# Edge stage of a graph layer on one Trainium2 core: edges sorted on the chip by tile of targets, sums in SBUF, a hand-ordered pipeline of quads and pairs

## The chip, the cores and the metric

One core of a Trainium2 chip runs the whole program. TensorE (PE), VectorE (DVE), ScalarE (ACT), GpSimd (POOL) and SyncE (SP) each work through a list of instructions of their own, in order, and wait for each other by semaphores. SP, ACT and POOL issue DMAs; only POOL issues the indirect ones, in which an index per partition chooses a row in DRAM. The metric is the device time of one execution in microseconds (us), the median of several runs.

## What is computed

x holds 3125 nodes of 512 features; 50000 edges run from src to dst (edge attributes: 32 numbers, and 4 called sh). Three parts follow each other: x plus a graph layer plus a linear attention, both of layernorm(x); then x plus a mixture of 8 experts (2 for each node). The graph layer's edge part, cut to what matters:

```python
pre = irrep_linear(x, W_pre0, b_pre0, W_pre1)          # p0: 128, p1: 3 x 128 features
ip1 = einsum('eum,eum->eu', p1[edge_dst], p1[edge_src]) / 3.0
s0 = concatenate([p0[edge_dst], p0[edge_dst], ip1], -1)
w = ssp(edge_attr @ W_f1) @ W_f2 * (ssp(s0 @ W_s1) @ W_s2)   # ssp: softplus - log 2; 4 x 128
x0e, x1e = split_irreps(x[edge_src]);  sh0, sh1 = edge_sh[:, 0], edge_sh[:, 1:4]
out0 = w1 * x0e * sh0 + w4 * (sum(x1e * sh1) / sqrt(3.0))
out1 = w2 * x0e * sh1 + w3 * x1e * sh0
out = segment_sum(merge(out0, out1), edge_dst, 3125) + self_x
```

(The layer is called with edge_index = (src, dst), so the program's src is the row that an edge adds to, its target, and dst the row that it reads.)

## The kernel before, in words

The program has three stages, each in a block with pools of its own: the dense stage (L121), the edge stage (L357) and the expert stage (L502). A scheduler orders the instructions of each engine. N is 3125 (NT = 25 tiles of 128 nodes), T is 392 tiles of 128 edges.

**Dense stage.** x is loaded into `base`, normalised and transposed into xT (L177 to L185); POOL adds a bias to base (L182). POOL also zeroes the sums in DRAM (L196) and copies the expert weights into row order (w_rows, 32 DMAs of 1 MB, L207). Then, in chunks of 512 nodes, each tile gets a row `r` of 1312 numbers (L256 to L277): p0 through W_s1 (32), p1 (384) and the node's own transformed features (512). They are written to two DRAM tables: rows_d (416 numbers, read by target) and rows_s (896, read by source); the own features also start the sums acc[0]. The loop of keys and values follows (ps_k, ps_v, ps_kv, L292 to L307; POOL's memset of v at L302), then queries, z and the output projection (L318 to L352).

**Edge stage.** 98 groups of G = 4 edge tiles. For each tile POOL gathers 128 rows of rows_d (gd, L400) and of rows_s (gx, L404). A group compares its targets with each other (sel, L416) and moves repeated targets of a tile to spare rows (at, L425). DVE multiplies p1 of both ends (prod, L429); PE transposes and adds the products by 12 matmuls with the identity (ps_ip, L433) and makes both hidden layers (ps_h, L442 to L446); ACT and DVE apply ssp (hid, L454). For each tile then: two matmuls of 32 rows by 512 (wa L460, wb L462), the weights wt (L465 to L467), the features ft on DVE (L472 to L486), a matmul with sel that adds edges of one target (ps_s, L491), a copy to `so`, and an indirect DMA that adds so to one of two DRAM accumulators (L494).

**Expert stage.** Both accumulators are loaded and added (ac, L569), projected and added to base; then come the gates, the sorting of tokens by expert, and 56 slots of 128 tokens (L798 to L846).

Of the kernel before, what the change touches and what calls it, by code (L numbers as in the profile page):

```python
# [8 lines left out]
F32 = mybir.dt.float32  # L9
# [9 lines left out]
MUL = 128  # L19
G = 4  # L20
NACC = 2
# [14 lines left out]
def gnn_mix_moe_kernel(ctx: ExitStack, tc: tile.TileContext, a: dict, out: bass.AP):  # L36
# [11 lines left out]
    NPAD = (N + P + P - 1) // P * P  # L48
# [11 lines left out]
    keep = ctx.enter_context(tc.tile_pool(name="keep", bufs=1))  # L60
    dram = ctx.enter_context(tc.tile_pool(name="dram", bufs=1, space=DRAM))


    base = keep.tile([P, NT, D], F32, name="base")
    nc.vector.memset(base[:, NT - 1, :], 0.0)
    for t in range(NT):
        nc.sync.dma_start(base[: tn(t), t, :], a["x"][t * P : t * P + tn(t), :])
# [6 lines left out]
    before = const.tile([P, P], F32, name="before")  # L74
    nc.vector.tensor_scalar(before, jp, 0.0, None, op0=ALU.is_lt)
# [3 lines left out]
    nc.vector.memset(half, 0.5)  # L79

# [3 lines left out]
    acc = [dram.tile([NPAD, D], F32, name=f"acc{k}") for k in range(NACC)]  # L84
# [4 lines left out]
    def layer_norm_stats(pool):  # L89

        mv = pool.tile([P, NT, 2], F32, name="mv")
        nc.vector.memset(mv, 1.0)
        for t in range(NT):
            n = tn(t)
            st = pool.tile([P, 6], F32, name="bn", bufs=3)
            nc.vector.bn_stats(st[:n], base[:n, t, :])
            nc.vector.bn_aggr(mv[:n, t, :], st[:n])
        rs = pool.tile([P, NT], F32, name="rs")
        nc.scalar.activation(rs, mv[:, :, 1], AF.Sqrt, bias=eps)
        nc.vector.reciprocal(rs, rs)  # L100
        return mv, rs

    def normalise(dst, t, mv, rs):
        n = tn(t)
        nc.vector.tensor_scalar(
            dst[:n], base[:n, t, :], mv[:n, t, 0:1], rs[:n, t : t + 1],
            op0=ALU.subtract, op1=ALU.mult,
        )

    def transpose_rows(dst, src, t, psum):  # L110

        n = tn(t)
        ps = psum.tile([P, 4, P], F32, name="ps_t", tag="mm")
        for b in range(4):
            nc.tensor.transpose(ps[:, b, :n], src[:n, b * P : (b + 1) * P], ident[:n, :n])
        nc.scalar.copy(dst[:, :, t * P : t * P + n], ps[:, :, :n])
# [4 lines left out]
    with ExitStack() as c1:  # L121
        w = c1.enter_context(tc.tile_pool(name="w1", bufs=1))
        big = c1.enter_context(tc.tile_pool(name="big1", bufs=1))
        work = c1.enter_context(tc.tile_pool(name="work1", bufs=2))
        psum = c1.enter_context(tc.tile_pool(name="psum1", bufs=4, space=PSUM))
# [51 lines left out]
        mv, rs = layer_norm_stats(w)  # L177
        for t in range(NT):
            n = tn(t)
            xn = work.tile([P, D], F32, name="xn")  # L180
            normalise(xn, t, mv, rs)
            added = nc.gpsimd.tensor_add(base[:n, t, :], base[:n, t, :], b_add[:n])  # L182
            nc.vector.tensor_add(base[:n, t, :], base[:n, t, :], xn[:n])
            transpose_rows(xT, xn, t, psum)

        zero = w.tile([P, 2 * D], F32, name="zero")
        nc.gpsimd.memset(zero, 0.0)
        with tc.issue_after(added.ins):  # L190
            for k in range(NACC):
                r0 = N if k == 0 else 0
                while r0 < NPAD:
                    left = NPAD - r0
                    n, r = (min(2 * P, left), 2) if left % 2 == 0 else (1, 1)
                    nc.gpsimd.dma_start(  # L196
                        acc[k][r0 : r0 + n, :].rearrange("(p r) d -> p (r d)", r=r),
                        zero[: n // r, : r * D],
                    )
                    r0 += n  # L200


        with tc.issue_after(added.ins):
            for e in range(NE):
                for l in range(NL + 1):
                    src = a["Wh"][e, l] if l < NL else a["Wo"][e]
                    nc.gpsimd.dma_start(  # L207
                        w_rows[l][e * P : (e + 1) * P, :].rearrange("p (k f) -> p k f", k=4),
                        src.rearrange("(k p) f -> p k f", p=P),
                    )  # L210
# [3 lines left out]
        for c in range(NCH):  # L214
            m = cn(c)
            cols = slice(c * CH, c * CH + m)
            sq = work.tile([P, 3, CH], F32, name="sq", tag="wide")
            nc.vector.tensor_mul(sq[:, :, :m], xT[:, 1:4, cols], xT[:, 1:4, cols])
            nc.vector.tensor_add(sq[:, 0, :m], sq[:, 0, :m], sq[:, 1, :m])
            nc.vector.tensor_add(sq[:, 0, :m], sq[:, 0, :m], sq[:, 2, :m])  # L220
            rooted = nc.scalar.activation(n1[:, cols], sq[:, 0, :m], AF.Sqrt, scale=1.0 / 3.0)


        for c in range(NCH):
# [27 lines left out]
            for t in tiles_of(c):  # L252
# [24 lines left out]
                nc.sync.dma_start(acc[0][rows, :], r[:n, x0:])  # L277
# [40 lines left out]
        for c in range(NCH):  # L318
# [10 lines left out]
            for t in tiles_of(c):  # L329
# [12 lines left out]
                )  # L342
                pt = psum.tile([P, 4, P], F32, name="ps_zt", tag="mm")
# [8 lines left out]
                nc.vector.tensor_add(base[:n, t, :], base[:n, t, :], po[:n])  # L352
# [3 lines left out]

    with ExitStack() as c2:  # L357
        w = c2.enter_context(tc.tile_pool(name="w2", bufs=1))
        gat = c2.enter_context(tc.tile_pool(name="gat", bufs=3))
        work = c2.enter_context(tc.tile_pool(name="work2", bufs=2))  # L360
        ps1 = c2.enter_context(tc.tile_pool(name="ps1", bufs=1, space=PSUM))
        ps2 = c2.enter_context(tc.tile_pool(name="ps2", bufs=2, space=PSUM))


        to_i = w.tile([P, T], I32, name="to_i")
        nc.sync.dma_start(to_i, a["src_t"])
        of_i = w.tile([P, T], I32, name="of_i")
        nc.sync.dma_start(of_i, a["dst_t"])
        sh = w.tile([P, T, 4], F32, name="sh")
        nc.sync.dma_start(sh, a["sh_t"])  # L370
        w_f1 = w.tile([HID, HID], F32, name="w_f1")
        nc.scalar.dma_start(w_f1, a["W_f1"])
        w_s1c = w.tile([P, HID], F32, name="w_s1c")
        nc.scalar.dma_start(w_s1c, a["W_s1"][2 * MUL :, :])

        w_fs = w.tile([2 * HID, D], F32, name="w_fs")
        nc.scalar.dma_start(w_fs[:HID], a["W_f2"])
        nc.scalar.dma_start(w_fs[HID:], a["W_s2"])

        to_f = w.tile([P, T], F32, name="to_f")  # L380
        nc.vector.tensor_copy(to_f, to_i)

        spare_i = w.tile([P, 1], I32, name="spare_i")
        nc.gpsimd.iota(spare_i, pattern=[[0, 1]], base=N, channel_multiplier=1)
        spare = w.tile([P, 1], F32, name="spare")
        nc.vector.tensor_copy(spare, spare_i)
        away = w.tile([P, T], F32, name="away")
        nc.vector.tensor_scalar(away, to_f, spare, -1.0, op0=ALU.subtract, op1=ALU.mult)
# [4 lines left out]
        isq3 = 1.0 / math.sqrt(3.0)  # L393
        for g in range(T // G):
            gs = slice(g * G, (g + 1) * G)
            gd = gat.tile([P, G, HID + 3 * MUL], F32, name="gd")
            gx = gat.tile([P, G, 3 * MUL + D], F32, name="gx")
            for i in range(G):
                t = g * G + i
                nc.gpsimd.indirect_dma_start(  # L400
                    out=gd[:, i, :], out_offset=None, in_=rows_d[:, :],
                    in_offset=bass.IndirectOffsetOnAxis(ap=to_i[:, t : t + 1], axis=0),
                )
                nc.gpsimd.indirect_dma_start(  # L404
                    out=gx[:, i, :], out_offset=None, in_=rows_s[:, :],
                    in_offset=bass.IndirectOffsetOnAxis(ap=of_i[:, t : t + 1], axis=0),
                )
            row = gat.tile([P, G, P], I32, name="row")
            nc.sync.dma_start(row.rearrange("p g j -> p (g j)"), _rows(a["src_row"][g * G * P :], P, G * P))
            ea = gat.tile([HID, G * P], F32, name="ea")  # L410
            nc.sync.dma_start(ea, a["edge_attr"][:, g * G * P : (g + 1) * G * P])

            sel = work.tile([P, G, P], F32, name="sel")
            nc.vector.tensor_tensor(  # L416
                sel, row, to_f[:, gs].unsqueeze(2).to_broadcast([P, G, P]), op=ALU.is_equal
            )
            dup = work.tile([P, G, P], F32, name="dup")
            nc.vector.tensor_mul(dup, sel, before.unsqueeze(1).to_broadcast([P, G, P]))  # L420
            cnt = work.tile([P, G], F32, name="cnt")
            nc.vector.tensor_reduce(cnt, dup, AX.X, ALU.add)
            nc.vector.scalar_tensor_tensor(cnt, cnt, 0.0, away[:, gs], op0=ALU.is_gt, op1=ALU.mult)
            at = work.tile([P, G], I32, name="at", bufs=3)
            nc.vector.tensor_add(at, cnt, to_f[:, gs])  # L425


            prod = work.tile([P, G, 3 * MUL], F32, name="prod")
# [511 lines left out]
```

## Time and profile before

| what | us |
|---|---|
| median of 3 runs (3865.62 to 3876.13) | 3869.45 |
| the profiled execution, its own time | 3855.79 |
| its span, first to last instruction | 3854.0 |
| dense stage: start to the last output projection (L351) | 0 to 643.5 |
| first gather of the edge stage (L400) | 646.1 |
| first and last indirect add to DRAM (L494) | 693.8, 2791.7 |
| expert stage: first matmul (L572), first of the slots (L820) | 2801.9, 3009.6 |

How to read the profile: the page gives each engine's busy time, the span in 40 slices (a digit is a busy share in tenths; PEclk is the TensorE clock that was granted, in tenths of full speed), and groups of instructions with their line, count, busy time, mean ns of one, and the idle time just before them with what ended it ("issue": nothing that the profile shows). "x392" is a count; "PEld" is TensorE's loading of a stationary operand. DMA-issuing on POOL counts as busy only for the indirect and direct DMAs' own instructions.

### The profile page before, as it was taken

To read this page: it belongs to the slowest core of one execution; us is meant where nothing else is said; L and a number is where in the kernel's file an instruction comes from. 1 tells how busy PE (TensorE), PEld (TensorE's weight loads), DVE (VectorE), ACT (ScalarE), POOL (GpSimd) and SP (SyncE) were. 2 spreads that over 40 slices of the span, in tenths; PEclk is the share of its full clock that TensorE was granted. 3 is DMA by queue.
4 is the path that set the end of the run, shared out by engine and by line. 5 is a ranking of instruction groups with operands and counts; after the bars stand their busy time and mean duration, and the time that the engine had idled before them with its cause. 6 is when DMAs were issued, how large, how long until landed. Compare 5 with 4: busy or idle time off the path is not lost. (4 is left out here: it accounts for less than half of the span.)

```text
span 3854.0 us, 45302 instructions
## 1 busy us (share of the span) xinstructions
PE 3360.6 (87%) x14722; PEld 2072.1 (54%) x14722; DVE 2199.5 (57%) x6167; ACT 1153.5 (30%) x2596; POOL 2192.2 (57%) x1678
## 2 busy tenths in 40 slices
PE   3579986889898989898989898989857899999998
PEld 2346543444444444444444444444442788888887
DVE  6311233688787888787878787878774222222221
ACT  1111110344444444444444444444310111111111
POOL 3300002688888878888887788887601344444442
PEclk8789998677777777777777777777775899999999
DMA  3790002678888888887878878888655215184550
GB/s 123 283 362 17 0 0 97 157 178 193 185 188 191 187 195 188 194 189 191 187 191 187 195 182 197 188 193 184 128 166 222 62 53 184 53 320 154 194 185 23
DMA packets 222731, 632.23 MB, mean 164 GB/s; under 512 B 53019, under 2 KB 57936, under 8 KB 211744
## 3 DMA queue, kind: packets, MB, share of 16 engines
q0 software_dynamic: 169328, 535.41, 53.5%
q1 hardware_dynamic: 43978, 81.76, 6.7%
q10 hardware_dynamic: 9190, 12.18, 0.9%
q8 instruction: 117, 1.92, 0.2%
q14 instruction: 118, 0.97, 0.1%
HBM read 619.43 MB, written 193.83 MB: 211 GB/s over the span
## 5 line engine op out<-in xcount | busy, mean ns | idle before, releaser
L494 POOL DMA_INDIRECT acc<-so,at x392 | 804.8, 2053 | 198.5 <-issue 119.9
L460 PE MATMUL wa<-w_fs,hid 32*128 32x512 f32 x784 | 648.8, 999 | 201.0 <-issue 104.0
L462 PE MATMUL wb<-w_fs,hid 32*128 32x512 f32 x784 | 712.0, 1038 | 1.7
L491 PE MATMUL ps_s<-ft,sel 128*128 128x512 f32 x784 | 542.5, 781 | 0.9 <-DVE ft L486 0.9
L404 POOL DMA_INDIRECT gx<-rows_s,of_i x392 | 469.1, 1197 | 119.5 <-issue 74.7
L400 POOL DMA_INDIRECT gd<-rows_d,to_i x392 | 434.4, 1108 | 124.0 <-issue 107.0
L433 PEld LDWEIGHTS ps_ip<-ident,prod 128*128 128x128 f32 x2352 | 395.1, 248 | 169.9 <-issue 169.9
L460 PEld LDWEIGHTS wa<-w_fs,hid 32*128 32x128 f32 x784 | 206.2, 274 | 518.0 <-issue 301.5
L829 DVE TENSOR_SCALAR h<-ps_f,bias 128x128 f32<-128x128 f32 x336 | 117.1, 350 | 558.1 <-PE ps_f L820 541.3
L772 POOL DMA_INDIRECT we<-w_rows,w_at x224 | 230.6, 1030 | 349.3 <-PE ps_f L820 130.3
L820 PE MATMUL ps_f<-h,we 128*128 128x128 f32 x3584 | 424.1, 277 | 4.0 <-ACT h L827 4.0
L820 PEld LDWEIGHTS ps_f<-h,we 128*128 128x128 f32 x3584 | 408.8, 192 | 7.5 <-ACT h L827 6.1
L493 ACT COPY so<-ps_s 128x512 f32<-128x512 f32 x392 | 227.7, 581 | 559.7 <-PE ps_s L491 524.5
L433 PE MATMUL ps_ip<-ident,prod 128*128 128x128 f32 x2352 | 384.4, 328 | 11.2 <-DMA ea<-in_edge_attr 8.3
L486 DVE SCALAR_TENSOR_TENSOR ft<-wt,sh,ft 128x128 f32<-128x128 f32 x1176 | 340.1, 343 | 0.0
L827 ACT ACTIVATE h<-ps_f,bias 128x128 f32<-128x128 f32 x336 | 121.4, 367 | 663.9 <-PE ps_f L820 570.5
L465 ACT ACTIVATE wt<-wa,sh 128x256 f32<-128x256 f32 x392 | 186.5, 476 | 424.1 <-PE wb L462 197.7
L473 DVE SCALAR_TENSOR_TENSOR dot<-gx,sh,dot 128x128 f32<-128x128 f32 x392 | 135.0, 344 | 259.1 <-ACT dot L472 91.7
L491 PEld LDWEIGHTS ps_s<-ft,sel 128*128 128x128 f32 x784 | 145.7, 232 | 249.6 <-DVE ft L479 114.3
L467 DVE TENSOR_TENSOR wt<-wt,wb 128x512 f32<-128x512 f32 x392 | 265.5, 677 | 5.4 <-PE wb L462 2.9
L462 PEld LDWEIGHTS wb<-w_fs,hid 32*128 32x128 f32 x784 | 185.2, 275 | 103.7 <-DVE wt L467 90.1
L820 PEld LDWEIGHTS ps_f<-xt,we 128*128 128x128 f32 x1792 | 210.5, 193 | 27.5 <-issue 27.0
(237 smaller groups left out, 4791.9 us busy)
## 6 DMA issues: line engine op xcount, KB each, us to landing
row<-in_src_row SPq DMA_DIRECT2D x98, 256.0 KB
w_rows<-in_Wh POOLq DMA_DIRECT2D x24, 1024.0 KB
ac<-acc SPq DMA_DIRECT2D x48, 256.0 KB
rows_s<-r SPq DMA_DIRECT2D x24, 448.0 KB
w_rows<-in_Wo POOLq DMA_DIRECT2D x8, 1024.0 KB
acc<-zero POOLq DMA_DIRECT2D x13, 512.0 KB
ea<-in_edge_attr SPq DMA_DIRECT2D x98, 64.0 KB
gd<-rows_d,to_i POOLq DMA_INDIRECT x392
```

The lines of the kernel that those rows point to most:

```text
L400: nc.gpsimd.indirect_dma_start(out=gd[:, i, :], out_offset=None, in_=rows_d[:, :], in_offset=bass.IndirectOffsetOnAxis(ap=to_i[:, t : t + ...
L404: nc.gpsimd.indirect_dma_start(out=gx[:, i, :], out_offset=None, in_=rows_s[:, :], in_offset=bass.IndirectOffsetOnAxis(ap=of_i[:, t : t + ...
L433: nc.tensor.matmul(ps_ip[:, i * P : (i + 1) * P], prod[:, i, b * P : (b + 1) * P], ident, start=(b == 0), stop=(b == 2),)
L460: nc.tensor.matmul(wa, hid[:HID, es], w_fs[:HID], start=True, stop=True)
L462: nc.tensor.matmul(wb, hid[HID:, es], w_fs[HID:], start=True, stop=True)
L467: nc.vector.tensor_mul(wt, wt, wb)
L486: nc.vector.scalar_tensor_tensor(ft[:, b, :], w2, sh[:, t, b : b + 1], ft[:, b, :], op0=ALU.mult, op1=ALU.add)
L491: nc.tensor.matmul(ps_s, sel[:, i, :], ft.rearrange("p b u -> p (b u)"), start=True, stop=True)
L493: nc.scalar.copy(so, ps_s)
L494: nc.gpsimd.indirect_dma_start(out=acc[i % NACC][:, :], out_offset=bass.IndirectOffsetOnAxis(ap=at[:, i : i + 1], axis=0), in_=so, in_offs ...
L772: nc.gpsimd.indirect_dma_start(out=dst, out_offset=None, in_=src, in_offset=bass.IndirectOffsetOnAxis(ap=at[:, j : j + 1], axis=0), bounds ...
L820: nc.tensor.matmul(pss[f], ws[l][:, k, f * P : (f + 1) * P], h[:, k, :], start=(k == 0), stop=(k == 3))
```

## The change

Edges are sorted into slots by tile of targets at the start of the dense stage: DVE counts the edges of each tile of 128 targets (25 compares and 25 scans over 392 columns), PE adds over partitions, and DVE works out a place for every edge. Each tile starts on a new pair (2 x 128 slots); NPR = 220 pairs, or NQ = 110 quads of 512 slots, cover the worst case, empty slots being zero. For each of 14 chunks of 28 edge tiles, a record of 40 numbers per edge is built (sh, both row numbers, place in the tile, and ssp(edge_attr @ W_f1)), and POOL puts each tile of records to its slots in DRAM by an indirect DMA (392 puts, after 10 DMAs that clear the records). The record tiles have two buffers. base is no longer kept: x plus its norm goes to `out` and is loaded again (y). The w_rows DMAs go from POOL's queue to SP's. In the edge stage all edges of a pair belong to one tile of 128 targets, so the one-hot matmul yields sums for that tile, which DVE adds to `acc` in SBUF at a tile number read from pair_tile; the indirect adds to DRAM and the search for repeated targets are gone. The products go to POOL, three multiplies of each tile from DVE to ACT, and the features of a tile take two matmuls instead of one. The order of PE, ACT, DVE and POOL in this stage is written out by hand. In the expert stage, own features and x come by two loads in place of the two accumulators'.

In the built order of instructions, POOL's 392 puts all stand ahead of its 25 memsets of v. On DVE the record writes of all 14 chunks stand ahead of the row stage's second chunk (xg, r), the layernorm of x between those of chunks 2 to 9. On PE the row stage, keys and values, and queries follow each other as before.

```diff
+    NPR = (T * P - NT) // (PR * P) + NT
+    NQ = (NPR * PR + G - 1) // G
...
+            rec = chk.tile([P, CT, REC], F32, name="rec")      # chk: bufs=2
...
+            for i in range(CT):
+                put = nc.gpsimd.indirect_dma_start(
+                    out=recs[:, :], out_offset=bass.IndirectOffsetOnAxis(ap=at_i[:, t : t + 1], axis=0),
+                    in_=rec[:, i, :], in_offset=None,
+                )
...
-                    nc.gpsimd.dma_start(
-                        w_rows[l][e * P : (e + 1) * P, :].rearrange("p (k f) -> p k f", k=4),
+                nc.sync.dma_start(
+                    w_rows[l][e * P : (e + 1) * P, :].rearrange("p (k f) -> p k f", k=4),
...
-                nc.sync.dma_start(acc[0][rows, :], r[:n, x0:])
...
+    acc = keep.tile([P, NT, D], F32, name="acc")
...
+        def fetch(q, k):                       # rec by SP; gd: bufs=3, gx: bufs=5
+            for i in (2 * k, 2 * k + 1):       # two indirect DMAs on POOL for each tile
+                nc.gpsimd.indirect_dma_start(
+                    out=Q.gd[:, (i + 2) % G, :], out_offset=None, in_=rows_d[:, :],
+                    in_offset=bass.IndirectOffsetOnAxis(ap=reci[:, i, 5:6], axis=0),
+                )
...
+        def products(q):
+            for k in range(2):
+                g = slice(2 * k, 2 * k + 2)
+                nc.gpsimd.tensor_mul(
+                    Q.prod[:, g, :], Q.gd[:, g, HID:], Q.gx[:, 2 - 2 * k : 4 - 2 * k, : 3 * MUL]
+                )
+        def turn(q):                           # 12 transposes into ps_ip, adding; ACT copies to ip
+        def hidden(q):                         # 4 matmuls, ip stationary, w_s1c moving (32 columns)
+            nc.vector.tensor_copy(Q.h1, Q.rec[:, :, 8:])
+            nc.vector.tensor_add(Q.h, ps, Q.gd[:, :, :HID])
+        def softplus(q):                       # Abs, Exp, Ln on ACT over 128 columns; one op on DVE
+        def turn_hidden(q):                    # 2 transposes; ACT copies to hT
+        def weigh(s):
+            wa = ps_w.tile([P, PR, D], F32, name="wa")         # ps_w: bufs=1
+            wb = ps_w.tile([P, PR, D], F32, name="wb")
+            for k, i in enumerate(tiles):      # rows 32 i to 32 i + 31
+                nc.tensor.matmul(wa[:, k, :], Q.hT[r, 0, :], w_f2[r, :], start=True, stop=True)
+            for k, i in enumerate(tiles):      # the other two strips of 32 rows
+                nc.tensor.matmul(wb[:, k, :], Q.hT[r, 1, :], w_s2[r, :], start=True, stop=True)
+            for k, i in enumerate(tiles):
+                nc.scalar.activation(
+                    R.wt[:, k, : 2 * MUL], wa[:, k, : 2 * MUL], AF.Copy, scale=Q.rec[:, i, 0:1]
+                )
+            nc.scalar.copy(R.wt[:, :, 2 * MUL :], wa[:, :, 2 * MUL :])
+            nc.vector.tensor_mul(R.wt, R.wt, wb)
+        def dots(s):                           # 2 scaled copies on ACT
+        def dots2(s):                          # 4 scalar_tensor_tensor on DVE
+        def which(s):                          # one compare on DVE, 2 x 128 columns
+        def feats(s):
+            nc.vector.tensor_mul(R.au, w2, x[:, :, :MUL])
+            for k, i in enumerate(tiles):
+                for c in range(1, 4):
+                    nc.scalar.activation(
+                        R.ft[:, k, 1, c * MUL : (c + 1) * MUL], R.au[:, k, :], AF.Copy, scale=Q.rec[:, i, c : c + 1]
+                    )
+            nc.vector.tensor_mul(R.ft[:, :, 0, :MUL], w1, x[:, :, :MUL])
+            nc.vector.tensor_mul(
+                R.ft[:, :, 0, MUL:].rearrange("p k (b u) -> p k b u", b=3),
+                x[:, :, MUL:].rearrange("p k (b u) -> p k b u", b=3),
+                w3.unsqueeze(2).to_broadcast([P, PR, 3, MUL]),
+            )
+            nc.vector.tensor_mul(R.ft[:, :, 1, :MUL], w4, R.dot)
+        def gather_up(s):
+            for k in range(PR):
+                for m in range(2):
+                    nc.tensor.matmul(
+                        ps, R.one[:, k, :], R.ft[:, k, m, :], start=(k == 0 and m == 0), stop=(k == 1 and m == 1)
+                    )
+            b = nc.vector.value_load(pair_tile[0:1, s : s + 1], min_val=0, max_val=NT - 1)
+            nc.vector.tensor_add(sums, sums, ps)               # sums: acc[:, b, :]
+            LEAD = 9
+            for s in range(-LEAD, NPR):        # due(n): the quad that begins at pair s + n, if one does
+                fetch((s + LEAD) // PR, (s + LEAD) % PR)
+                for q in due(6): products(q)
+                dots(s + 1); which(s + 1); weigh(s + 1)
+                for q in due(2): turn_hidden(q)
+                for q in due(3): softplus(q)
+                for q in due(5): turn(q)
+                dots2(s + 1); feats(s + 1)
+                if s >= 0: gather_up(s)
+                for q in due(4): hidden(q)
...
-                for k in range(NACC):
-                    nc.sync.dma_start(ac[:n, k, :], acc[k][t * P : t * P + n, :])
+                own = work.tile([P, 2, D], F32, name="own", bufs=2)
+                nc.sync.dma_start(own[:n, 0, :], rows_s[t * P : t * P + n, 3 * MUL :])
+                nc.sync.dma_start(own[:n, 1, :], out[t * P : t * P + n, :])
```

(The comments stand for lines that are left out; dots and dots2 work as L472 to L474 do, on the tiles of a pair.)

## The prediction

> **What bounds the kernel now.** I read the slices first. The edge stage fills slices 7 to 29 (646 to 2792 us, 56% of the span). PE is nearly full there, but at a granted clock of 0.7, and POOL shows only 8.
>
> ```profile
> PE   3579986889898989898989898989857899999998
> DVE  6311233688787888787878787878774222222221
> POOL 3300002688888878888887788887601344444442
> PEclk8789998677777777777777777777775899999999
> ```
>
> The groups (mean ns of one) and POOL's timeline tell more.
>
> ```profile
> L494 POOL DMA_INDIRECT acc<-so,at x392 | 804.8, 2053 | 198.5 <-issue 119.9 <-ACT so L493 25.0 <-DMA acc<-so,at 22.6
> L404 POOL DMA_INDIRECT gx<-rows_s,of_i x392 | 469.1, 1197 | 119.5 <-issue 74.7 <-DVE dot L473 19.2 <-DVE ft L486 12.8
> L400 POOL DMA_INDIRECT gd<-rows_d,to_i x392 | 434.4, 1108 | 124.0 <-issue 107.0 <-DMA acc<-so,at 4.0 <-PE wb L462 4.0
> L843 POOL DMA_INDIRECT out<-r,out_at x56 | 57.5, 1026 | 116.2 <-DVE r L842 74.8 <-DVE h L829 30.1 <-issue 11.2
> ```
>
> ```profile
> 1799.55 0.95 POOL L400 DMA_INDIRECT gd<-rows_d,to_i  x1 [0.30 <-issue]
> 1800.80 0.95 POOL L400 DMA_INDIRECT gd<-rows_d,to_i  x1 [0.30 <-issue]
> ...
> 1805.24 3.45 POOL L494 DMA_INDIRECT acc<-so,at  x1 [0.30 <-issue]
> ```
>
> Ahead of every indirect DMA stand 0.30 us in which POOL waits for nothing. So a group of four tiles costs POOL 4 x (1.108 + 1.197 + 2.053) + 12 x 0.305 = 21.1 us. From the first add (693.8) to the last (2791.7) there are 97.75 groups of 21.46 us: **POOL is full to 98%**, and it bounds the edge stage. PE's 90% is work stretched by a half clock:
>
> ```profile
> 1804.50 0.94 PE L460 MATMUL wa<-w_fs,hid 32*128 32x512 f32 x1 [1.91 <-issue]
> 1804.51 0.94 PE L462 MATMUL wb<-w_fs,hid 32*128 32x512 f32 x1
> 1805.24 1.05 PE L460 MATMUL wa<-w_fs,hid 32*128 32x512 f32 x1
> 1806.09 1.05 PE L460 MATMUL wa<-w_fs,hid 32*128 32x512 f32 x1
> ```
>
> Passes start 0.85 apart here, 0.44 at a clock of 1.0 (8 passes of ps_y, 512 columns each, start to next start 3.54 us). wa and wb start together: two strips of 32 rows work side by side.
>
> **Ahead of the edge stage.** Sort on DVE: loads to 6 us; 25 x (compare 0.35, scan 0.95, scalar_tensor_tensor 0.55) = 46, between the rows of 200 columns (0.27, 0.57, 0.37) and 1.03 ns for each element more (DVE multiplies: 128 columns 285 ns, 384 columns 549); a reduction over 9800 elements, 10; small ones 14. First put at 76 us. If scans cost half or twice this, 64 to 100.
>
> A put is an indirect write that adds nothing. The nearest row is L843, 1.026; L400 alone is the floor, 0.95; the adding one, 2.05, is the ceiling. With 0.305: **1.33** (1.26 to 2.36). I take L843, the one that also only writes rows. The records have two buffers and DVE works in order, so the rows after the first chunk wait until the puts of chunk 11 of 0 to 13 are through: 76 + 12 x 28 x 1.33 + 3 (landing) = 526 us (502 to 872). Layernorm goes on between the chunks, under the puts. What is left then: the rest of chunk 1 of the row stage 13, four chunks of 20 (266 to 286 us in the trace, when the weight copies had ended; 28 under them), the last one 5; keys and values 156 (291.5 to 447.7) and queries to projection 197 (446 to 643.5), both PE-bound at clock 1.0; 2.5 to the first gather. 526 + 98 + 156 + 197 + 2.5 = **980 us in place of 646: +334**. The memsets of v behind the last put (76 + 392 x 1.33 = 597) are done before keys and values need them at 624. The weight copies, now on SP between the edge attributes, cost 4.8 us each (32 in 131 to 285); the last ten go out at about 390 and end at 440, under the puts, else the four chunks take 28: +32. The loads and stores of y hide under 7.9 us for each tile. Lost: about 43 us of POOL's bias adds and the 15 zeroing DMAs, which were on no path after 300 us: 0.
>
> **The edge stage, for each quad (110 of them).** POOL: 8 gathers at 1.10 (0.96 alone; the DVE's two-input work raised them to 1.15) + 0.305 = 11.2. Two multiplies of 768 columns: the add of 512 shows 1.27 alone and 1.67 beside DVE, and slows DVE too:
>
> ```profile
> 43.07 1.27 POOL L182 TENSOR_TENSOR base<-base,b_add 128x512 f32<-128x512 f32 x1 [41.01 <-DVE xn L105]
> ...
> 67.29 3.33 POOL L182 TENSOR_TENSOR base<-base,b_add 128x512 f32<-128x512 f32 x2 [1.69 <-DVE xn L105]
> ```
>
> ```profile
> 69.43 2.33 DVE L183 TENSOR_TENSOR base<-base,xn 128x512 f32<-128x512 f32 x2 [1.17 <-POOL base L182]
> ```
>
> (DVE's two take 2.33, not 2 x 0.68: the second stands still while POOL adds.) So 1.9 to 2.5 each, 2.25 taken: POOL **15.9** (14.0 to 16.8). The indirect adds, 9.4 of the 21.1, are gone.
>
> PE at full clock: weigh 2 x 0.85 (four strips side by side, else 3.4), gather_up 16 passes x 0.43 = 6.8, 12 transposes x 0.11 (ps_zt: four in 0.44) = 1.3, hidden and its turns 1.2: 11.0. DVE for a pair: wt 1.14, dots2 1.05, which and three multiplies of 256 columns 4 x 0.34, that of 768 0.87, the add to acc 0.60; with the quad's 0.7: 10.7. ACT 9.5. The loop that ACT and DVE close for a pair: wt copies 1.33, DVE wt 1.14, dots2 1.05, au 0.42, six scaled copies 1.8, the next dots 0.6, and 0.1: 6.45; with softplus' op 13.2 a quad, and some 2 more where POOL's multiplies lock DVE out: 15.2. gd's three buffers make another loop: a fetch waits for hidden of three quads before, whose products then need 15.9 (POOL) + 1.15 (DVE's wait after POOL's add) + turn 1.3 + gather_up 3.6 + add 0.7 + one pair 6.5 = 29 for two quads, 14.6 each.
>
> value_load: no row shows one. Below 0, above the 1.17 us in which DVE waits after POOL (a result fetched from elsewhere): 220 x 1.17 = 257. I take 0: four multiplies (1.9 us) are queued ahead of it, and the add behind it waits for PE anyway; only the scale is unlike. The Trainium skill, "DMA: Bandwidth & Descriptors", section "Latency and other measured facts", gives a tensor_load a floor of about 600 ns: 132 us if nothing hid it. No run here shows it.
>
> Three loops lie within 10% of each other, where before POOL's stood alone and was met to 2%. I take 4% above the largest: **16.6 us a quad**. From the first gather to the first sum: 16 gathers 21, multiplies 5, the chain behind them 19: 45 (47.7 before). Edge stage 45 + 109.5 x 16.6 = 1863 (2146 before): **-283**.
>
> **Behind it.** 2791.7 to the end, 1062. The 10 us in which the last add lands go; own tiles have two buffers in place of three, a tile 3.15 for 2.9: +6. Taken: **1058** (1050 to 1075).
>
> **Sum.** 980 + 1863 + 1058 = 3901 us of span against 3854, with the 1.8 around it 3903 against 3855.8, **+1.2%**. The median is 14 us above the profiled execution, so the same sum on its scale is 3917; I forecast between, 3910. Even is at 16.2 a quad.
>
> **Clock, against the change.** PE must wait some 2 us a pair. After the idle 1.91 above, passes ran at half clock for 10 us. If such gaps cool it here, PE needs up to 22 us a quad and is the bound. I count it mostly warm: the cold passes used 64 rows of the array, gather_up uses 128 and is dense. The Trainium skill, "TensorE: Matmul & The Clock Gate", section "Why this matters for your kernels", says that only idle gaps above some 3 us throttle. The row, 1.91 us, differs. By the page PE stays at 11.0 and the sum is unchanged; by the row the last rival below decides.
>
> **Rivals.**
> 1. *POOL keeps its own pace* (faster). If the loops don't meet, the edge stage runs at 14.0 to 16.0 a quad: at 15.0 the stage is 45 + 1643 and the time 3728. For it: POOL ran at 98% before, and its adds are gone. Against it: the two other loops. It decides below 16.1.
> 2. *Puts cost like adds*, or wait for landings under the weight copies: at 1.9 each 980 becomes 1171 and the time 4094. For it: L494; against it: L843.
> 3. *POOL's multiplies shut DVE out*: at 19 a quad the time is 4165. For it: L183's 2.33. Against: wt and acc's add read PSUM.
> 4. *PE cold*: at 22 a quad the time is 4494.
>
> That sums don't reach acc, and DRAM adds remain, is excluded by the built program.
>
> **Chances.** The forecast's case (16.0 to 17.6 a quad, 3837 to 4012) 0.43; rival 1, 0.36; rival 2, 0.10; rival 3, 0.07; rival 4, 0.04. 0.3%, about what this measurement can tell from no change, is 12 us (0.11 us a quad each way): of the forecast's case 0.06 lies within it, 0.01 under it. Faster 0.37, same 0.06, slower 0.57. The range: below, puts at 1.28 and 14.6 a quad, 3670; above, rival 3 with a later start, 4190. Under it a tenth of the chance, above it a tenth; the forecast's own case is 3837 to 4012.
>
> **What would show it.** First gather at 980; puts 1.33 apart, and DVE's record writes waiting for them; POOL's share in the edge stage near 0.8, its gaps 0.30; last add to acc near 2840; clock above 0.8 there. A first gather before 900 or after 1050, or a quad outside 16.0 to 17.6, makes this wrong.

## The result, and the profile after

The changed kernel takes 4159.23 us (median of 4 runs, 4151.83 to 4168.89) against 3872.79 before (4 runs): a ratio of **1.0737**, 95% interval 1.0698 to 1.0776. Forecast were 3910 us, +1.2%; the direction is right, the size is not. The profiled run has a span of 4161.0 us, 260 above the sum of 3901.

| | forecast | profile after |
|---|---|---|
| first, last put (L238) | 76, 597 | 83.1, 705.8 |
| row stage ends (L395) | 624 | 795.2 |
| keys and values | 156 | 156 |
| queries to the last projection | 197 | 207 |
| first gather (L549) | 980 | 1170.8 |
| first, last add to acc (L700) | 1025, 2843 | 1231.2, 3083.5 |
| one quad | 16.6 | 16.92 |
| behind the last add | 1058 | 1077.5 |

So 191 us of the 260 stand ahead of the edge stage, 50 in it, 19 behind it. The slices of the changed kernel (each 104 us) show the place:

```profile
PE   2112223998847888888888778787875799999998
DVE  7212200213348888888888888888866222222221
POOL 2655765000068787778888887777711044444443
PEclk9999856999969889888998998989997599999999
```

In slices 1 to 6 (104 to 728 us) PE is idle for 75% and DVE for 83% of the time, and POOL, which should have been the pace, is busy for only 60%. The edge stage (slices 12 to 28) is near what was counted: POOL at 7 to 8, with 0.30 us ahead of each of its gathers but the first of a quad (1.04), and PE's clock near 0.9. The groups (count | busy, mean ns | idle before, and what ended it):

```profile
L238 POOL DMA_INDIRECT recs<-rec,at_i x392 | 388.7, 991 | 306.5 <-issue 117.6
L549 POOL DMA_INDIRECT gd<-rows_d,rec x440 | 537.3, 1221 | 470.4 <-issue 235.2
L553 POOL DMA_INDIRECT gx<-rows_s,rec x440 | 549.0, 1248 | 137.7 <-issue 131.6
L564 POOL TENSOR_TENSOR prod<-gd,gx 128x768 f32<-128x768 f32 x220 | 395.8, 1826 | 2.7 <-DMA gx<-rows_s,rec 0.9
L588 DVE COPY h<-rec 128x128 f32<-128x128 f32 x110 | 287.1, 2610 | 0.0
```

A put costs 0.99 and 0.30 ahead of it, below the 1.33 forecast. So the puts alone would have ended near 590; something held their records back. ACT's waits between 80 and 720 us (total, times, longest) say what:

```profile
ACT sp L227 <- remote: 235.1, 11, 41.4
ACT sp L227 <- PE ps_h L220: 71.0, 10, 31.3
ACT rs L317 <- DVE mv L314: 51.4, 1, 51.4
ACT xT L328 <- remote: 38.7, 7, 9.0
```

"remote" is a wait that no recorded event ends. What these instructions wait for is PE. Its timeline, then POOL's and ACT's, around one of them:

```profile
188.39 4.29 PE L220 MATMUL ps_h<-w_f,ea 32*128 32x32 f32 x45 [10.63 <-issue]
192.84 0.21 PE L220 MATMUL ps_h<-w_f,ea 32*128 32x32 f32 x1 [0.16 <-issue]
194.25 0.44 PE L220 MATMUL ps_h<-w_f,ea 32*128 32x32 f32 x3 [1.20 <-issue]
196.37 1.15 PE L220 MATMUL ps_h<-w_f,ea 32*128 32x32 f32 x4 [1.69 <-issue]
199.21 0.64 PE L220 MATMUL ps_h<-w_f,ea 32*128 32x32 f32 x3 [1.70 <-issue]
```

```profile
243.18 0.97 POOL L238 DMA_INDIRECT recs<-rec,at_i  x1 [0.31 <-issue]
```

```profile
251.13 0.54 ACT L227 ACTIVATE sp<-ps_h 128x448 f32<-128x448 f32 x1 [41.39 <-remote]
```

PE's last product of the chunk is recorded at 199.9; ACT gets it at 251.1, 7 us after the last put of the chunk that POOL had under way (244.15), and SP's next load of edges, which waits for the same products, leaves at 251.12. From 192.8 to 199.9 the products trickle, one to four at a time; from there to 251.1 PE's record has nothing but four transposes at 208.2. While POOL streams puts, **PE's results come late**; then ACT, DVE and SP stand, and at last POOL runs out of records.

### The profile page after: what moved, and what is told of

Its sections match the earlier page's. It is cut to its first block, busy times and chain, and to the rows that moved or that the text cites. A ratio compares the mean times of both kernels' runs of the same rounds, so it can differ in the third digit from the quotient of the medians.

```text
span 4161.0 us, 45298 instructions
## 1 busy us (share of the span) xinstructions
PE 3061.2 (74%) x15082; PEld 1943.8 (47%) x15082; DVE 2164.1 (52%) x4149; ACT 1460.2 (35%) x3823; POOL 2281.4 (55%) x1931
## 5 line engine op out<-in xcount | busy, mean ns | idle before, releaser
L695 PE MATMUL ps_s<-ft,one 128*128 128x512 f32 x1760 | 906.9, 663 | 34.9 <-DVE ft L682 33.6
L549 POOL DMA_INDIRECT gd<-rows_d,rec x440 | 537.3, 1221 | 470.4 <-issue 235.2
L553 POOL DMA_INDIRECT gx<-rows_s,rec x440 | 549.0, 1248 | 137.7 <-issue 131.6
L695 PEld LDWEIGHTS ps_s<-ft,one 128*128 128x128 f32 x1760 | 367.9, 221 | 430.9 <-issue 373.4
L678 ACT ACTIVATE ft<-au,rec 128x128 f32<-128x128 f32 x1320 | 409.9, 389 | 439.7 <-DVE au L675 229.3
L238 POOL DMA_INDIRECT recs<-rec,at_i x392 | 388.7, 991 | 306.5 <-issue 117.6
L1002 POOL DMA_INDIRECT we<-w_rows,w_at x224 | 229.7, 1025 | 366.5 <-PE ps_f L1050 129.2
L564 POOL TENSOR_TENSOR prod<-gd,gx 128x768 f32<-128x768 f32 x220 | 395.8, 1826 | 2.7 <-DMA gx<-rows_s,rec 0.9
L634 DVE TENSOR_TENSOR wt<-wt,wb 128x1024 f32<-128x1024 f32 x220 | 267.4, 1216 | 178.9 <-ACT wt L633 150.0
L651 DVE SCALAR_TENSOR_TENSOR dot<-gx,rec,dot 128x128 f32<-128x128 f32 x880 | 297.2, 397 | 0.0
L588 DVE COPY h<-rec 128x128 f32<-128x128 f32 x110 | 287.1, 2610 | 0.0
```

Source lines behind the costliest of these rows:

```text
L238: put = nc.gpsimd.indirect_dma_start(out=recs[:, :], out_offset=bass.IndirectOffsetOnAxis(ap=at_i[:, t : t + 1], axis=0), in_=rec[:, i, :] ...
L549: nc.gpsimd.indirect_dma_start(out=Q.gd[:, (i + 2) % G, :], out_offset=None, in_=rows_d[:, :], in_offset=bass.IndirectOffsetOnAxis(ap=reci ...
L553: nc.gpsimd.indirect_dma_start(out=Q.gx[:, i, :], out_offset=None, in_=rows_s[:, :], in_offset=bass.IndirectOffsetOnAxis(ap=reci[:, i, 4:5 ...
L564: nc.gpsimd.tensor_mul(Q.prod[:, g, :], Q.gd[:, g, HID:], Q.gx[:, 2 - 2 * k : 4 - 2 * k, : 3 * MUL])
L588: nc.vector.tensor_copy(Q.h1, Q.rec[:, :, 8:])
L634: nc.vector.tensor_mul(R.wt, R.wt, wb)
```

## Experiments

Theories: **A**, the stream of puts makes PE late. **B**, the weight copies on SP's queue hold the edge loads. **C**, it is only the order and two record buffers. For the edge stage **P**, the DVE copy that POOL's products hold back costs the time, and **L**, the products on POOL do, whatever they hold. There were chips 0, 3 and 7, on which the kernel before took 3852.24 to 3882.51, 3833.95 and 3888.13. Which chip the profile above is from is not recorded. "Late" is the sum of ACT's "remote" waits from 80 to 900 us (322 in the profile above). e1, e2, e3 and wide_aside leave out part of the records, so of these the front alone is read. "Last put" is the last indirect DMA of that stream, whatever it moves.

| run | chip | last put | row stage ends | first gather | quad | late | time |
|---|---|---|---|---|---|---|---|
| e1_no_puts | 0 | - | 447 | 817 | 17.01 | 0 | 3814.6 |
| e2_reads | 0 | 725 | 789 | 1158 | 17.01 | 255 | 4164.8 |
| e3_half_rows | 0 | 772 | 859 | 1228 | 16.98 | 305 | 4222.8 |
| e4_w_rows_pool | 0 | 741 | 815 | 1184 | 16.99 | 298 | 4186.4 |
| e5_h1_act | 3 | 588 | 616 | 983 | 16.95 | 0 | 3970.5 |
| e6_block | 3 | 592 | 621 | 993 | 16.99 | 0 | 3984.9 |
| e7_wide | 3 | 622 | 625 | 994 | 16.94 | 0 | 3976.0 |
| after_again | 7 | 690 | 779 | 1152 | 16.98 | 276 | 4151.6 |
| block_again | 7 | 650 | 744 | 1113 | 16.95 | 243 | 4108.6 |
| e10_dve_products | 7 | 698 | 788 | 1161 | 13.81 | 238 | 3812.6 |
| e11_all | 7 | 889 | 578 | 1087 | 13.75 | 206 | 3729.0 |
| after_third | 0 | 680 | 771 | 1141 | 17.01 | 288 | 4144.7 |
| wide_again | 0 | 750 | 816 | 1186 | 17.01 | 249 | 4188.7 |
| wide_aside | 0 | 751 | 813 | 1181 | 16.98 | 280 | 4178.8 |
| spaced | 0 | 1042 | 457 | 1260 | 17.00 | 0 | 4263.4 |
| spaced_less | 0 | 716 | 605 | 989 | 16.99 | 0 | 3985.6 |

**What the puts cost.** `if i: continue` ahead of the put.

> Leaves out 364 of the 392 puts (only the first of each chunk of 28 stays), so most records never reach DRAM and most gathers read row 0; only the front is read from this run. In the changed kernel the first gather starts at 1170.8 us and the row stage ends at 795. Theory A (while puts are in flight, PE gets on only by single matmuls and its results are told late, and everything waits for PE): the front falls to its dense work, row stage over by 430 at the latest, first gather between 750 and 830, and the 30 to 45 us waits of ACT for ps_h are gone. Theory B (the weight copies on SP's queue hold the edge loads): waits of the same length stay, first gather later than 1050. Theory C (two record buffers and queues in program order, with no harm from the puts but their own time): as A, since the chunk no longer waits for puts.

First gather 817, nothing late. The puts cost 324 us of the front against the unaltered kernel on the same chip (after_third, 1141), 354 against the profile above. A and C live; B would have kept the waits.

**Direction, number of rows, weight copies.**

```diff
-  out=recs[:, :], out_offset=..., in_=rec[:, i, :], in_offset=None       # e2: 27 of 28
+  out=rec[:, i, :], out_offset=None, in_=recs[:, :], in_offset=...
-  in_=rec[:, i, :]                                                       # e3
+  in_=rec[:64, i, :]
-  nc.sync.dma_start(w_rows[l] ...)                                       # e4
+  nc.gpsimd.dma_start(w_rows[l] ...)
```

> In place of 364 puts, as many indirect gathers of the same size (128 rows of 160 bytes from the record array into the record tile), at the same places of POOL's queue with the same waits; the records do not reach DRAM. POOL's time stays at about 1.27 us each. Theory A in the form 'small writes to DRAM do it': PE is free, the row stage ends with the last of these (by my old sum near 624), first gather at 970 to 1010. Theory A in the form 'any indirect DMA of so many small rows does it': first gather stays at 1130 to 1200. Theory C (POOL's own pace and the order): 1130 to 1200 too, but without single matmuls 2.6 us apart on PE.

> Each put writes the records of 64 of the 128 partitions (the other half of the records stays away from DRAM). Theory A, by the number of small writes in flight: the waits of ACT for ps_h fall to about a half (235 us of them in the changed kernel), row stage over at 600 to 680, first gather 980 to 1060. Theory C: the front shortens only as POOL's own time for a put does (0.97 us busy before).

> Only the queue of the 32 weight copies changes: back from SP to POOL's, nothing left out. Theory B (they hold SP's edge loads): first gather near 980, total 3970 to 4000. Theory A: first gather 1120 to 1220, total within 50 us of 4159; their issues cost POOL some 30 us.

None frees PE. Reads do the same as writes, 64 rows the same as 128 (no shorter, even longer), and B falls: 1184.

**The held copy; fewer PE instructions; wider rows.**

```diff
-  nc.vector.tensor_copy(Q.h1, Q.rec[:, :, 8:])                           # e5
+  nc.scalar.copy(Q.h1, Q.rec[:, :, 8:])
-  nc.tensor.matmul(ps[:, r, ...], ea[rows, tile i], w_f1[rows, :])       # e6, 4 of these
+  nc.tensor.matmul(ps[:, 4 tiles], ea[:, tile i], w_f1)  # 128 x 128, block-diagonal
-  in_=rec[:, i, :]                                                       # e7, recs 120 wide
+  in_=rec[:, i : i + 3, :]
```

> Only the copy of the edge part of a quad's hidden rows goes from DVE to ACT; nothing is left out. In the changed kernel that copy is held 2610 ns while POOL multiplies, the add behind it frees the gd buffer late, and POOL sits 1.04 us before the quad's first gather instead of 0.30. Theory P (that held copy costs the stage): the gap falls to 0.30, a quad takes 16.0 to 16.4 us instead of 16.92, total 4070 to 4110. Rival (POOL would have been late anyway, or DVE's other work is held instead): a quad at 16.7 or more, total within 25 us of 4159.

> Four 32-row products of an edge chunk become one 128-row product against a block-diagonal weight: the same records from a quarter of PE's instructions (98 products instead of 392), the same puts; edge tiles are loaded in runs of 512 bytes; nothing is left out. Theory A (under a stream of puts PE gets on by one instruction in about 0.7 us, so that what counts is the number of PE's instructions): PE keeps up with the puts, its idle time put down to issue (160 us ahead of ps_h) nearly goes, the row stage ends at 620 to 690, first gather 985 to 1060. Theory C (order and two buffers): first gather within 40 us of 1171.

> The same puts, but each row is 480 bytes instead of 160 (a record and the two behind it, in a record array three times as wide; only the first 160 bytes are read later); nothing of the result is left out. The zeros to be written first are three times as many, so that the first put moves from 83 to about 140. If the smallness of the rows slows PE: ps_h's waits for issue go, first gather 1000 to 1070. If it is the stream of indirect DMAs whatever their size: first gather 1190 to 1260 (57 us later, for the zeros).

P falls: the quad stays at 16.95. The lockout only takes the next DVE instruction, as the two groups show, `one` in the changed kernel and in e5:

```profile
L661 DVE TENSOR_TENSOR one<-lane,rec 128x256 f32<-128x256 f32 x220 | 95.2, 433 | 0.0
```

```profile
L661 DVE TENSOR_TENSOR one<-lane,rec 128x256 f32<-128x256 f32 x220 | 276.3, 1256 | 0.0
```

But e5's front is the changed kernel's, and it took 983 us instead of 1171. Its waits of ACT over the same time have no "remote":

```profile
ACT sp L227 <- PE ps_h L220: 211.8, 15, 29.1
ACT r L401 <- DVE r L400: 58.9, 16, 24.2
```

The order and the two buffers are the same in e5, so C alone doesn't explain the 188 us. And e6 and e7 told nothing there: no run on chip 3 had a late PE (nor e9, the edits of e5 and e6 together: first gather 990, 3978.8 us).

**The unaltered kernel again; products on DVE; records spread.**

> The changed kernel once more, unaltered, beside the others of this call. The run with only the edge stage's copy moved (whose front is the changed kernel's, instruction by instruction) had its first gather at 983 us instead of 1171 and its last put at 588 instead of 706. If the front's long time belongs to the chip that a run is on (chip 0 in the first call, chip 3 in the second), this run shows either front in company with all others of the call: 975 to 1000, or 1150 to 1190. If it belonged to the kernel's own text, it is 1150 to 1190 here whatever the others do.

> The kernel with the block-diagonal product once more, beside the changed kernel on one chip. Where the changed kernel's first gather is near 1171: theory A gives 985 to 1060 here, theory C 1130 or more. Where the changed kernel has 975 to 1000, both are within 25 us of each other, since POOL's puts at 1.29 us apart set the front then.

On chip 7 PE is late for the unaltered kernel, and a quarter of ps_h's instructions saves 39 us, not the 92 or more that A in its first form (0.7 us for each PE instruction) gave. That form falls. The lateness moves rather than goes: ACT's unexplained waits for ps_h drop from 198 to 53 us, those at xT and r (L324 and L388 there) rise from 69 to 190.

```diff
-  nc.gpsimd.tensor_mul(Q.prod[:, g, :], ...)                             # e10
+  nc.vector.tensor_mul(Q.prod[:, g, :], ...)
+  if t in {1: 2, 7: 3, 13: 4, 19: 5, 24: 6}: records(...)   # e11: layernorm; so too in the
+                                   # row stage (7 to 9) and keys and values (10 to 13)
```

> Only the two products of a quad (128x768 each, 1826 ns on POOL) go to DVE; nothing is left out. Theory L (POOL is full with 16.0 of 16.9 us a quad, and its products shut a DVE instruction out for 2.4 us a quad): POOL falls to some 12.3 us; DVE has 14.3 busy + 1.2 of queue work - 2.4 of lockout + 2 x 0.95 = 15.0 and becomes the bound: a quad at 15.0 to 15.8, total 120 to 200 us below the changed kernel on the same chip. Rival (PE, 13.6 us busy with its waits, or the chain ACT to DVE, sets the pace): a quad at 16.5 or more.

> Block-diagonal product, products on DVE, and the 14 chunks of records spread by hand over the dense stages (two at the start, five among layernorm, three among the row stage, four among keys and values), so that no dense instruction stands behind a chunk that waits for puts; nothing is left out. If the order is what the puts cost (the run without puts had its first gather at 816): first gather at 800 to 860, a quad as in the run with products on DVE, total 3600 to 3720, below the kernel before. If PE under puts is what costs, first gather 950 or later.

The products on POOL were the edge stage's price: 13.81 us a quad instead of 16.98, below the 15.0 to 15.8 that L gave, and 339 us off the time (3.17 x 109.5 = 347), where L gave 120 to 200. L's direction is shown, its sum is not. Groups of e10:

```profile
L564 DVE TENSOR_TENSOR prod<-gd,gx 128x768 f32<-128x768 f32 x220 | 200.8, 953 | 88.6 <-issue 65.9 <-DMA gx<-rows_s,rec 22.2
L588 DVE COPY h<-rec 128x128 f32<-128x128 f32 x110 | 38.1, 346 | 0.0
```

A product is 0.95 on DVE, 1.83 on POOL, and the copy that POOL held for 2.61 takes 0.35: for DVE the work of two products is paid by the lockout that goes. e10 takes POOL's own 3.7 us and the lockout away together, so that how the 3.2 us a quad divide between them is not shown; moving the held copy alone (e5) gained nothing. PE's clock rises from 0.89 to 1.00 as well, and PE is 90% busy there, DVE 89%: which of them now sets the pace is open. e11 takes 84 us more off, less than hoped: the dense stages now run under the puts, and PE is late there too.

**Size of the rows.** As e7; and 27 of 28 puts with 1600-byte rows to an array of their own.

> The changed kernel unaltered, as the mark of this call: on chips 0 and 7 the first gather came at 1152 to 1184 us and ACT had 170 to 235 us of waits for PE that no event in the trace ends; on chip 3 the same front had its first gather at 983 and none of these. One of the two is expected, whole: first gather 975 to 1000 with no such waits, or 1140 to 1190 with them.

> The puts with rows of 480 bytes instead of 160, nothing left out, beside the changed kernel on one chip. If the changed kernel's first gather is late here: with the theory that the smallness of the rows slows PE, first gather at 1000 to 1070 and no unexplained waits of ACT; with any stream of indirect DMAs, at least as late as the changed kernel's. If the changed kernel is at 975 to 1000, this tells nothing new and gives 990 to 1010.

> 27 of 28 puts write rows of 1600 bytes into an array that is never read (most records do not reach DRAM): the same 128 rows a put and the same 1.27 us of POOL, ten times the bytes, near what the edge stage's gathers move. Where the changed kernel's front is late: if the size of the rows is what matters (the gathers of the edge stage have 1664 and 3584 bytes and PE is not late there), first gather 960 to 1020; if not, 1140 to 1190. Where the changed kernel is at 975 to 1000: the same within 25 us.

Chip 0, all late: the size of the rows is not it, nor is it a matter of puts alone. The kernel before has one such wait too, where its edge stage begins and POOL issues 24 gathers 1.27 us apart (646 to 679 us); PE's record of the transposes ends at 668.8, and ACT has their result at 675.3. The second line is ACT's:

```profile
663.69 5.08 PE L433 MATMUL ps_ip<-ident,prod 128*128 128x128 f32 x24 [8.31 <-DMA ea<-in_edge_attr]
675.33 0.60 ACT L438 ACTIVATE ip<-ps_ip 128x512 f32<-128x512 f32 x1 [16.92 <-remote]
```

e10 shows the same at its own start, under 32 gathers 1.25 us apart (1161 to 1202 us), after PE's transposes ended by 1188.9:

```profile
1200.11 0.59 ACT L579 COPY ip<-ps_ip 128x512 f32<-128x512 f32 x1 [11.83 <-remote]
```

**Density.**

```diff
+  pause = nc.gpsimd.memset(idle, 0.0)   # behind each put; idle: 400 columns (600, twice, in spaced)
```

> After each put POOL clears a scratch tile of 600 columns twice (and the tiny clears of v go from POOL to DVE, so that they don't stand between puts); nothing is left out. POOL's puts come some 2 to 3 us apart instead of 1.27, so the front gets longer whatever PE does: last put at 900 to 1250. What is read is PE under the puts: the changed kernel had 170 to 235 us of ACT's waits for ps_h that no event ends, on chips 0 and 7. If a dense stream of puts makes PE late: these waits fall below 60 us here. If any indirect DMA in flight does: they stay above 150 us, or grow with the longer time. On a chip like chip 3 there are none in either case.

> The same with one scratch clear of 400 columns after each put, puts some 1.7 to 2.0 us apart, near the mean pitch of the gathers in the edge stage (1.72 with products on DVE), where PE is not late on any chip. If the density of the stream decides: unexplained waits of ACT for ps_h below 100 us, last put at 700 to 850. If not: 150 us or more, last put at 800 or later.

Chip 0 again, where PE was late for the unaltered kernel (after_third), though after_third did not run side by side with these two. ACT's waits for ps_h in after_third, then ACT's waits and POOL's groups in spaced_less:

```profile
ACT sp L227 <- remote: 205.4, 11, 53.7
ACT sp L227 <- PE ps_h L220: 70.8, 10, 29.4
```

```profile
ACT sp L229 <- PE ps_h L222: 176.3, 12, 29.4
ACT rs L323 <- DVE mv L320: 54.6, 8, 17.7
```

```profile
L241 POOL DMA_INDIRECT recs<-rec,at_i x392 | 393.1, 1003 | 135.6 <-DVE at_i L195 69.5 <-issue 65.6 <-DVE fm L429 0.2
L248 POOL MEMSET idle<- 128x400 f32 x392 | 177.8, 453 | 0.2
```

Nothing is late any more, with puts 1.59 us apart instead of 1.27. **178 us of work that is of no use make the kernel 159 us faster** (3985.6 against after_third's 4144.7) and put the first gather at 989. The scheduler also orders records and dense stages somewhat differently there, so part of the 159 may be order; that the unexplained waits go is not, since e11, with another order and dense puts, kept 206 us of them.

Two rivals remain. One is that chip 0 was simply not late that time, as chip 3 was not. Two marks speak against it. The slots of the expert stage are the same work in every run; from their first matmul to the end they took 841 to 842 us in chip 3's four runs, 844 to 851 in all others, and 849 and 848 in spaced and spaced_less. And only the pages of chip 3's runs give landing times of DMAs. Both marks may belong to the chip, though, rather than to its being late; an unaltered kernel side by side with the spaced ones would have settled it, and was not run.

The other is the recording. Those landing times are missing elsewhere because events are: of 16 for each DMA the trace keeps 99% in e5 and 60% in the changed kernel, and between 100 and 700 us 20% there, 78% in spaced_less. So where PE is late, events are lost too. Every run here was recorded, hence none can tell whether PE would be late without the recording.

**The version that beats both.** e11's kernel, timed four times:

> The version with block-diagonal product, products on DVE and records spread over the dense stages, three rounds against the kernel before. Products on DVE alone brought a quad from 16.98 to 13.81, which is 347 us over the stage. On a chip where PE is late under the puts: first gather 1070 to 1110, total 3710 to 3750, ratio 0.95 to 0.975. On one where it is not: first gather 800 to 880, total 3430 to 3520, ratio 0.89 to 0.92.

3729.69 us (3723.72 to 3741.42) against 3865.61: **0.9645**, 0.9614 to 0.9676, with PE still late (190 us). Spaced puts in this version were not run.

## Why the prediction was wrong, step by step

- *First put at 76, puts 1.33 apart:* 83.1, and 1.27 where nothing waits. Both within the stated bounds.
- *"Layernorm goes on between the chunks, under the puts"; 526 + 98 = 624 for the row stage:* **this step failed.** It took PE to run as usual under the puts; ended at 795, +171. On chip 3, where PE isn't late, the same row stage ended at 616 and the first gather came at 983 against 980 forecast. The counting of buffers, order and queues held there, though so close only by luck: -8 us up to the row stage's end and +11 behind it cancel. The cover was given no price. No stream of indirect DMAs ran beside the dense stage of before, but the start of its edge stage had the one wait of 16.92 us that no event ends, under gathers 1.27 us apart; the prediction doesn't look at it.
- *Keys and values 156, queries to projection 197, 2.5 to the first gather:* 156, 207, and 12.6, as on SP the first load of records waits 7.4 us for the last store of y and leaves only at 1167.6. +20 of it missed.
- *Rival 2 (puts like adds, 4094)* gave the right start (1171) by luck: the puts were cheap, 1.27 and not 1.9.
- *A quad: POOL 15.9, gathers 1.10, multiplies 2.25; 4% above that, 16.6:* the prediction's own terms add to 11.2 + 2 x 2.25 = 15.7, not 15.9. Measured: POOL 8 x (1.235 + 0.305) + 2 x 1.83 = 16.0, quad 16.92. That POOL's sum is nearly right is luck: gathers were 1.1 us a quad too cheap, multiplies 0.8 too dear. Fill 60, not 45. Together +50.
- *Rival 3 (multiplies shut DVE out):* the mechanism was there (2.61 for a copy), at 16.9 and not 19 a quad. Having the products on POOL at all cost e10's 3.2 us a quad, of which the lockout is a part that no run separates.
- *PE mostly warm:* right, 0.89 between 1500 and 2500 us. But its waits do cool it. PE waits for POOL's products 1.7 us on average and 5.0 at most, 2.55 in a typical quad; from 2003.2 to 2006.6, behind the wait below, the granted clock is 0.50:

```profile
2001.23 0.88 PE L574 MATMUL ps_ip<-ident,prod 128*128 128x128 f32 x6 [2.55 <-POOL prod L564]
```

  Between 1240 and 3000 us there are 90 such stretches of 3.4 or 6.8 us, 382 us in all; in e10, where no wait of PE between 1240 and 2700 us is over 1.3 us, there is none. The Trainium skill, "TensorE: Matmul & The Clock Gate", "Why this matters for your kernels", puts the limit at some 3 us; here 2.55 us, with 0.88 more behind them, were enough, as 1.91 was in my row of before.
- *value_load 0:* its parts on DVE's queue are shown by the lines of L698: a load of 304 ns, register work of 190 and 93, an assert of 23, 0.61 us for each pair. It was hidden: the load and register work run while DVE computes ft, and DVE goes from L682 to L687 without a gap, in e10 too (L682 from 1647.97 for 0.95 us, L687 at 1648.84). Right. The Trainium skill, "DMA: Bandwidth & Descriptors", "Latency and other measured facts", has a floor of about 600 ns for a tensor_load; the load's record here is half of that.
- *Behind, 1058:* 1077.5; from the last add to the first slot 230 us instead of 218. A tile of the loop with the two loads took 3.61 us instead of 2.90, which is 17 us, not 6.

## What to carry to other kernels

Work counted as hidden under another engine's stream must have been seen beside such a stream once; if no row shows it, the cover gets a range like any unknown cost. Look first at waits that no event ends, and at which engine they really wait for. Before giving elementwise work to POOL because DVE is full, add what DVE then loses while it is shut out: here two products of 0.95 us on DVE cost less than the 2.3 us lost at the copy, and POOL's 3.7 besides.

## What the runs showed of the hardware that was not expected

- In these recorded runs, a stream of indirect DMAs on POOL every 1.27 us makes TensorE's results late on chips 0 and 7, not on chip 3, whether it writes or reads, 64 or 128 rows, 160 to 1600 bytes each. At 1.59 us apart it doesn't (one run at that distance, one at a greater, both on chip 0). It shows at the start of the edge stage as well, in the kernel before (16.9 us) and in e10 (11.8 us), where gathers come 1.25 to 1.27 us apart; once the edge stage runs, with gathers 1.7 us apart on average in e10, no wait of ACT from 1240 us on is unexplained. Why the chips differ, by what path POOL's stream reaches PE, and whether the recording has a part in it, stays open.
- PE's clock went to half behind waits of 2.55 and 0.88 us (changed kernel) and of 1.91 us (before).
- While POOL multiplies, a DVE copy of 128 columns takes up to 4.0 us (mean 2.61, 0.35 without); moved to ACT, the next DVE instruction is held in its place.
